# Keys made by features and turned back, edge features in two loads, borders for two steps at once

## The chip, the cores and the metric

The kernel runs on one core of a Trainium2 chip. The metric is the device time of one execution in microseconds (us); it is the time of that one core. TensorE (PE) multiplies and transposes, VectorE (DVE) and ScalarE (ACT) work elementwise, GpSimd (POOL) issues gathers, SyncE (SP) issues most of the other DMAs. An engine runs its instructions in program order and waits on semaphores for the others.

## What is computed

A graph of 12,500 nodes with 128 features and 212,500 edges that are sorted by their destination `dst`. Each edge has 128 features of its own. The layer, cut to what matters:

```python
h = relu(layernorm(x))                                   # nodes
q = h @ Wq.T + bq ;  v = h @ Wv.T + bv                   # nodes, 8 heads x 16
k = edge_attr @ Wk.T + bk                                # edges
in_m, out_m, diag_m = sum(q[src]*k), sum(q[dst]*k), sum(q[src]*q[dst])   # per edge and head
score = (segsoftmax(in_m/4) + segsoftmax(out_m/4) + segsoftmax(diag_m/4)) * edge_weight**lam
att = segment_sum(score * v[dst], dst)                   # score, for each node, times v
y = x + leaky_relu(att @ Wo.T + bo)
```

`segsoftmax` is a softmax over the edges of one destination node. Since `v[dst]` is the same for all edges of a node, the kernel sums only the scores.

## The kernel before, in words

All of it is in `ordered_path`. A prologue (to about 156 us of the profile) computes q of all nodes into a table in DRAM and starts the first gathers. Then comes one long loop, `for g in range(end)` at L1694, of 415 steps. The sorted edges are cut into S = 5 segments of G = 83 blocks of 512 edges; step g is segment s = g % 5 of block row t = g // 5. So five steps make one t, and some work is done once a t. The node work that can already be done is fitted in between, and a last part finishes the nodes.

Program order is fixed by hand: each `pin` ties an instruction behind the one pinned before it on its engine. One step g issues, in this order:

- `gather(g + LOOK)`, POOL, L712: four indirect DMAs of 128 rows of q each, 26 steps ahead. The first waits for the PE instruction noted as `behind[g, 0]`, the third for `behind[g, 2]`; both were noted a step earlier. This only keeps the gathers close behind the products.
- `fetch_edges(g + EDGES)`, SP, L692: the features `ea` of one step (128 x 512 float32, 256 KB), six buffers.
- `turn(g + 2)`: four PE transposes of `ea` into `eT_ps` (L1266, one PSUM buffer), ACT's copy to `eT` (L1268, three buffers).
- `one_hots(g + 3)`: two ACT instructions (L703, L704) that make the one-hot matrix `oh` of the edges' destinations.
- `project(g + 1)`: four float32 matmuls with a piece of `eT` as the stationary operand and `wk` moving (L1274) and a bfloat16 matmul of three rows by 512 columns that adds the bias (L1275), into `k_ps` (two PSUM buffers). The trace has two records for each of these float32 matmuls and one for each transpose, and a weight load (PEld) for each record.
- `spread_q(g + 1)`: four bfloat16 matmuls (L1282) that spread q of the destinations into `qd_ps` (two PSUM buffers), and ACT's copy `qd` (L1285).
- `logits(g)` on DVE: `qq*k_ps` (L1293), `qq*qd_ps` (L1294), `qd*k_ps` (L1295) into one buffer `prod`, and the sum over each head's 16 features (L1296) into `lT`.
- by s, work once a t for the steps of one or two t before: scans for the softmax (L1356, L1384), one-hots of segment ends, `to_rows` (L1452, L1457) and so on, and two further queues in SP's order, `fetch_rows` (`win`, L686) and `put_rows` (`sums`, L1473). `fetch(t + 2)` issues `relb` (L665, 630 KB) and the segments' borders `far` (L670, 135 KB, four buffers) once a t.

At the end of a step, `behind[g + 1, 2]` is set to the last PE instruction so far.

Of the kernel before, what the change touches and what calls it, by code (L numbers as in the profile page):

```python
# [472 lines left out]
def ordered_path(ctx: ExitStack, tc: tile.TileContext, flag, x, src, dst, edge_attr, edge_weight,  # L473
# [104 lines left out]
    bq_all = consts.tile([P, F], F32, name="bq_all")  # L578
    pin(nc.scalar.dma_start(bq_all, bq[None, :].to_broadcast([P, F])))
# [18 lines left out]
    bv3, bk3, bo3 = [b3[:, i, None, :].to_broadcast([3, JN, F]) for i in range(3)]  # L598
# [3 lines left out]
    K4 = 1 + S * JN  # L602
    show_end = consts.tile([K4, S * JN], F32, name="show_end")
# [47 lines left out]
    qqs, st, eas, behind, base_v = {}, {}, {}, {}, {}  # L651
# [5 lines left out]
    def fetch(t):  # L657
# [9 lines left out]
        far = load.tile([R, FB], BF, name="far", bufs=4)  # L667
        lo = t * FB + HEAD
        of = bass.AP(far_d.tensor, far_d.offset + lo, [[G * FB, S], [0, H3], [1, FB]])
        pin(nc.sync.dma_start(far, of))  # L670
# [18 lines left out]
    def fetch_edges(g):  # L689
        if g < end:  # L690
            ea = eas[g] = load.tile([P, JN * F], F32, name="ea", bufs=EDGES)
            pin(nc.sync.dma_start(  # L692
                ea, edge_attr[:end * BE, :].rearrange("(s b p j) f -> p s b (j f)", s=S, b=G, p=P)
                [:, g % S, g // S, :]))
# [101 lines left out]
    with tc.tile_pool(name="prep", bufs=1) as prep, \  # L796
# [249 lines left out]
        for g in range(EDGES):  # L1046
# [211 lines left out]
    with tc.tile_pool(name="work", bufs=2) as work, \  # L1258
            tc.tile_pool(name="scan", bufs=2) as scan, \
            tc.tile_pool(name="ps", bufs=1, space=PSUM) as ps:  # L1260
        ks, eTs, qds, q_ps, lTs = {}, {}, {}, {}, {}

        def turn(g):
# [3 lines left out]
            eT = work.tile([P, JN, P], F32, name="eT", bufs=3)  # L1267
# [3 lines left out]
        def project(g):  # L1271
            k_ps = ks[g] = ps.tile([P, JN, F], F32, name="k_ps", bufs=2)
            for j in range(JN):
                pin(nc.tensor.matmul(k_ps[:, j, :], eTs[g][:, j, :], wk, start=(j == 0), stop=False))  # L1274
            pin(nc.tensor.matmul(k_ps, ones3, bk3, start=False, stop=True))  # L1275
            del eTs[g]

        def spread_q(g):
            s, d = g % S, st[g // S]
            qd_ps = q_ps[g] = ps.tile([P, JN, F], F32, name="qd_ps", bufs=2)  # L1280
# [7 lines left out]
        def logits(g):  # L1288
# [3 lines left out]
            prod = work.tile([P, JN, 3, F], F32, name="prod", bufs=1)  # L1292
            pin(nc.vector.tensor_mul(prod[:, :, 0, :], qqs[g], ks[g]))  # L1293
            pin(nc.vector.tensor_mul(prod[:, :, 1, :], qqs[g], q_ps[g]))  # L1294
# [395 lines left out]
        project(0)  # L1690
        spread_q(0)
        turn(1)
        raw_rectify(SOON)
        for g in range(end):  # L1694
# [4 lines left out]
            fetch_edges(g + EDGES)  # L1699
            if s == 1:  # L1700
                load_sources(t + IDX)
            if g + 2 < end:
                turn(g + 2)
# [166 lines left out]
```

## Time and profile before

| | |
|---|---|
| median of 3 timed runs | 2671.06 us (2661.86 to 2672.03) |
| profiled execution | 2660.3 us, of it 2658.5 us span |
| mean granted TensorE clock | 0.756 |
| DMA | 357.03 MB, mean 134 GB/s |
| first and last sum over heads (L1296) start | 156.0 and 2596.9 us |
| last gather of the loop | about 2476 us |

The profiled execution is one run; its time is 10.8 us below the median of the timed runs. In the rows, `x415` is a number of instructions; after the bar stand busy time and the mean of one, after the second bar the time that the engine sat idle just before them, and what ended most of that. "remote" is a release that the trace can't put down to an instruction, "issue" is time in which the engine waited for nothing that the profile shows. PEclk is the granted clock, 1.00 or 0.50 in a short window and something between as a mean. A release put down to a PE instruction that had ended long before means that the signal, and not the instruction, came last.

### The profile page before, as it was taken

The numbers are of one execution on the slowest core, as the hardware profiler recorded it, in microseconds if no ns is written. First come the engines' busy times: TensorE is split into PE (matmuls) and PEld (weight loads), VectorE is DVE, ScalarE is ACT, GpSimd is POOL, SyncE is SP. The second block draws the span as 40 slices with busy tenths as digits, with TensorE's granted clock in tenths as the row PEclk, the third lists the DMA queues.
The fourth block names the chain that finished last, engine by engine and source line by source line (L and its number), as shares of the span: only waits on it lengthen the run. The fifth ranks groups of instructions, "written<-read, shape, count | busy, mean of one in ns | idle before, by whom it ended". The sixth has DMA issues, their size and how long they took to land.

```text
span 2658.5 us, 37037 instructions
## 1 busy us (share of the span) xinstructions
PE 1895.1 (71%) x10956; PEld 1466.7 (55%) x10956; DVE 2032.3 (76%) x2813; ACT 1406.8 (53%) x2743; POOL 1584.0 (60%) x1680
## 2 busy tenths in 40 slices
PE   4657866677677767777777767767767687777785
PEld 2446655555455555555555556545655565555564
DVE  4648878777777877777778777777877777777995
ACT  3647745554455555554555555545555555554672
POOL 6655666666666666666666666666666666666100
PEclk6777877776777777777777777777777777677886
DMA  7655445445545555455445444554455445454431
GB/s 197 191 163 150 127 133 143 129 135 139 146 131 144 134 147 135 136 141 141 119 130 139 128 129 130 135 137 122 123 140 135 127 127 135 134 131 122 126 88 53
DMA packets 379583, 357.03 MB, mean 134 GB/s; under 512 B 193216, under 2 KB 299371, under 8 KB 379167
## 3 DMA queue, kind: packets, MB, share of 16 engines
q1 hardware_dynamic: 310637, 239.38, 32.5%
q0 software_dynamic: 53152, 108.92, 16.4%
q10 hardware_dynamic: 15584, 6.27, 1.0%
q8 instruction: 90, 1.47, 0.2%
q14 instruction: 120, 0.98, 0.1%
HBM read 322.10 MB, written 32.22 MB: 133 GB/s over the span
## 4 chain that ended last, share of the span: by engine, by line
PE 48%; issue 14%; ACT 14%; DVE 12%; another core or an unknown queue 10%; DMA 1%; DVEq 1%; POOL 0%; SPq 0%; ACTq 0%
PE k_ps L1274 13%; PE eT_ps L1266 8%; PE w_ps L1452 6%; PE qd_ps L1282 4%; PE k_ps L1275 4%; ACT eT L1268 3%; ACT qd L1285 2%; PE m_ps L1396 2%; DVE lT L1296 2%; PE node_ps L1205 2%; ACT relb L703 2%; DVE prod L1294 2%; DVE prod L1293 1%; PE d_ps L1438 1%
## 5 line engine op out<-in xcount | busy, mean ns | idle before, releaser
L712 POOL DMA_INDIRECT qq<-q_table,sources x1564 | 1480.3, 946 | 852.7 <-issue 355.1
L1296 DVE TENSOR_REDUCE lT<-prod 128x96 f32<-128x1536 f32 x415 | 727.5, 1753 | 14.3
L1274 PE MATMUL k_ps<-wk,eT 128*128 128x128 f32 x3320 | 613.6, 343 | 70.5 <-issue 41.0
L1274 PEld LDWEIGHTS k_ps<-wk,eT 128*128 128x128 f32 x3320 | 562.0, 254 | 99.0 <-issue 54.2
L1266 PE MATMUL eT_ps<-ident,ea 128*128 128x128 f32 x1660 | 352.7, 347 | 349.7 <-issue 226.9
L1285 ACT COPY qd<-qd_ps 128x512 f32<-128x512 f32 x415 | 239.4, 577 | 533.7 <-remote 164.3
L1266 PEld LDWEIGHTS eT_ps<-ident,ea 128*128 128x128 f32 x1660 | 243.5, 177 | 441.1 <-issue 269.5
L1293 DVE TENSOR_TENSOR prod<-qq,k_ps 128x512 f32<-128x512 f32 x412 | 280.5, 681 | 186.6 <-remote 55.4
L1268 ACT COPY eT<-eT_ps 128x512 f32<-128x512 f32 x415 | 242.7, 585 | 252.9 <-remote 125.2
L1294 DVE TENSOR_TENSOR prod<-qq,qd_ps 128x512 f32<-128x512 f32 x412 | 281.4, 683 | 100.8 <-ACT qd L1285 55.0
L703 ACT ACTIVATE relb<-relb,before 126x512 bf16<-126x512 bf16 x415 | 302.6, 729 | 0.0
L1295 DVE TENSOR_TENSOR prod<-qd,k_ps 128x512 f32<-128x512 f32 x415 | 282.2, 680 | 0.0
L1452 PE MATMUL w_ps<-back,sel 128*126 128x144 f32 (+1 forms) x1296 | 209.5, 325 | 95.0 <-ACT sel L1442 59.2
L704 ACT ACTIVATE oh<-relb 126x512 bf16<-126x512 bf16 x415 | 261.4, 630 | 13.2
L1452 PEld LDWEIGHTS w_ps<-back,sel 128*126 128x126 f32 (+1 forms) x1296 | 190.7, 218 | 106.0 <-ACT sel L1442 66.2
L1282 PE MATMUL qd_ps<-win,oh 126*128 126x128 bf16 x1660 | 194.8, 248 | 12.6 <-issue 12.4
L1275 PE MATMUL k_ps<-b,ones 3*128 3x512 bf16 x415 | 192.6, 464 | 4.7 <-issue 4.7
L1282 PEld LDWEIGHTS <-oh 126*128 126x128 bf16 x1660 | 109.2, 107 | 141.7 <-issue 141.4
L1405 DVE TENSOR_TENSOR back<-lT,m_ps 128x480 f32<-128x480 f32 x83 | 54.1, 651 | 98.3 <-remote 37.7
L1356 DVE TENSOR_TENSOR_SCAN l_ps<-far,carry,l_ps 120x512 f32<-120x512 bf16 x80 | 102.5, 1282 | 20.1 <-PE h_ps L1324 10.2
L1396 PE MATMUL m_ps<-ident,m 120*128 120x120 f32 x332 | 72.4, 349 | 52.7 <-issue 38.1
L712 POOL DMA_INDIRECT qq<-in_x_dram,sources x84 | 81.7, 973 | 42.8 <-issue 22.2
(237 smaller groups left out, 1811.1 us busy)
## 6 DMA issues: line engine op xcount, KB each, us to landing
ea<-in_edge_attr_dram SPq DMA_DIRECT2D x415, 256.0 KB
relb<-rel_d SPq DMA_DIRECT2D x83, 630.0 KB
qq<-q_table,sources POOLq DMA_INDIRECT x1564
win<-q_table SPq DMA_DIRECT2D x415, 31.5 KB
far<-far_d SPq DMA_DIRECT2D x84, 135.0 KB
q_table<-q SPq DMA_DIRECT2D x24, 384.0 KB
sums<-rows SPq DMA_DIRECT2D x411, 7.9 KB
q_table<-xq SPq DMA_DIRECT2D x24, 256.0 KB
```

The source lines that it names most:

```text
L703: pin(nc.scalar.activation(d, d, AF.Abs, bias=before[:K3]))
L712: rows = pin(nc.gpsimd.indirect_dma_start(out=qq[:, j, :], out_offset=None, in_=x if g < RAW else q_table, in_offset=bass.IndirectOffsetOn ...
L1266: pin(nc.tensor.transpose(eT_ps[:, j, :], eas[g][:, j * F:(j + 1) * F], ident))
L1268: pin(nc.scalar.copy(eT, eT_ps))
L1274: pin(nc.tensor.matmul(k_ps[:, j, :], eTs[g][:, j, :], wk, start=(j == 0), stop=False))
L1275: pin(nc.tensor.matmul(k_ps, ones3, bk3, start=False, stop=True))
L1282: pin(nc.tensor.matmul(qd_ps[:, j, :], ohs[g][:, j * P:(j + 1) * P], d["win"][:, s, :], start=(j == 0), stop=(j == JN - 1)))
L1285: pin(nc.scalar.copy(qds[g], qd_ps))
L1293: pin(nc.vector.tensor_mul(prod[:, :, 0, :], qqs[g], ks[g]))
L1294: pin(nc.vector.tensor_mul(prod[:, :, 1, :], qqs[g], q_ps[g]))
L1296: pin(nc.vector.tensor_reduce(lTs[t][:, :, s, :], prod.rearrange("p j i (h d) -> p j (i h) d", d=DIM), AX.X, ALU.add))
L1452: pin(nc.tensor.matmul(w_ps[:(hi - lo) * W, lo:hi].rearrange("p s c -> p (s c)"), d["sel"][:n, j, lo:hi, :].rearrange("p s w -> p (s w)"), ...
```

## The change

- **k by features.** `project` becomes one float32 matmul of 128 x 512 with `wk` as the stationary operand and all four pieces of `eT` moving, into a new PSUM tile `kT_ps` (features by edges). ACT copies it to SBUF and adds the bias, which is now one number a partition (`bk_col`). A new step `turn_back` turns the four pieces back with PE transposes into `k_ps`. The bias matmul is gone.
- **Order and buffers.** One iteration now issues `turn_back(g + 1)`, `one_hots(g + 3)`, `spread_q(g + 1)`, `project(g + 2)`, `turn(g + 3)`, `fetch_edges(g + 6)`, `logits(g)`. `behind[g + 1, 0]` is noted behind `spread_q`. PSUM has eight banks, so `qd_ps` goes from two buffers to one to make room for `kT_ps`; `eT` goes from three to two. DVE now does `qq*qd_ps` ahead of `qq*k_ps`.
- **Edge features.** In place of five loads a t there are two: segments 0 to 2 (768 KB) and 3 to 4 (512 KB), each into one buffer of its own.
- **Borders.** `far` is loaded for two t at once, three buffers.

```diff
+    EA = {0: 3, 3: 2}
...
     def fetch(t):
...
-        far = load.tile([R, FB], BF, name="far", bufs=4)
-        lo = t * FB + HEAD
-        of = bass.AP(far_d.tensor, far_d.offset + lo, [[G * FB, S], [0, H3], [1, FB]])
-        pin(nc.sync.dma_start(far, of))
+        if t % 2 == 0:
+            n = min(2, T - t)
+            fars[t // 2] = load.tile([R, 2, FB], BF, name="far", bufs=3)
+            lo = t * FB + HEAD
+            of = bass.AP(far_d.tensor, far_d.offset + lo, [[G * FB, S], [0, H3], [1, n * FB]])
+            pin(nc.sync.dma_start(fars[t // 2][:, :n].rearrange("r b f -> r (b f)"), of))
+        far = fars[t // 2][:, t % 2]
...
     def fetch_edges(g):
-        if g < end:
-            ea = eas[g] = load.tile([P, JN * F], F32, name="ea", bufs=EDGES)
+        if g < end and g % S in EA:
+            n = EA[g % S]
+            ea = load.tile([P, n, JN * F], F32, name=f"ea_{n}", bufs=1)
+            for i in range(n):
+                eas[g + i] = ea[:, i]
...
-            eT = work.tile([P, JN, P], F32, name="eT", bufs=3)
+            eT = work.tile([P, JN, P], F32, name="eT")
...
         def project(g):
+            kT_ps = ps.tile([P, JN, P], F32, name="kT_ps", bufs=1)
+            pin(nc.tensor.matmul(kT_ps.rearrange("f j p -> f (j p)"), wk,
+                                 eTs.pop(g).rearrange("f j p -> f (j p)"), start=True, stop=True))
+            kTs[g] = work.tile([P, JN, P], F32, name="kT")
+            pin(nc.scalar.activation(kTs[g], kT_ps, AF.Identity, bias=bk_col))
+
+        def turn_back(g):
             k_ps = ks[g] = ps.tile([P, JN, F], F32, name="k_ps", bufs=2)
             for j in range(JN):
-                pin(nc.tensor.matmul(k_ps[:, j, :], eTs[g][:, j, :], wk, start=(j == 0), stop=False))
-            pin(nc.tensor.matmul(k_ps, ones3, bk3, start=False, stop=True))
-            del eTs[g]
+                pin(nc.tensor.transpose(k_ps[:, j, :], kTs[g][:, j, :], ident))
+            del kTs[g]
...
-            qd_ps = q_ps[g] = ps.tile([P, JN, F], F32, name="qd_ps", bufs=2)
+            qd_ps = q_ps[g] = ps.tile([P, JN, F], F32, name="qd_ps", bufs=1)
...
+            pin(nc.vector.tensor_mul(prod[:, :, 1, :], qqs[g], q_ps[g]))
             pin(nc.vector.tensor_mul(prod[:, :, 0, :], qqs[g], ks[g]))
-            pin(nc.vector.tensor_mul(prod[:, :, 1, :], qqs[g], q_ps[g]))
...
         for g in range(end):
...
-            fetch_edges(g + EDGES)
...
+            if g + 1 < end:
+                turn_back(g + 1)
+                one_hots(g + 3)
+                spread_q(g + 1)
+                behind[g + 1, 0] = pinned[products]
             if g + 2 < end:
-                turn(g + 2)
-            one_hots(g + 3)
-            if g + 1 < end:
-                project(g + 1)
-                behind[g + 1, 0] = pinned[products]
-                spread_q(g + 1)
+                project(g + 2)
+            if g + 3 < end:
+                turn(g + 3)
+            fetch_edges(g + EDGES)
             logits(g)
```

How the instructions stand in program order, first on PE, in the middle of the loop of the kernel before. One step is the transposes (L1266), the keys (L1274, L1275) and the spread q (L1282); behind it comes a row of the once-a-t work.

```order
2993 L1266 MATMUL eT_ps<-ident,ea 128x128 x4
2994 L1274 MATMUL k_ps<-wk,eT 128x128 x4
2995 L1275 LDWEIGHTS ones_90
2996 L1275 MATMUL k_ps<-b_96,ones_90 128x512
2997 L1282 LDWEIGHTS oh
2998 L1282 MATMUL qd_ps<-win,oh 128x128
2999 L1282 LDWEIGHTS oh
3000 L1282 MATMUL qd_ps<-win,oh 128x128
3001 L1282 LDWEIGHTS oh
3002 L1282 MATMUL qd_ps<-win,oh 128x128
3003 L1282 LDWEIGHTS oh
3004 L1282 MATMUL qd_ps<-win,oh 128x128
```

The same place on PE in the changed kernel (its lines are numbered anew: L1290 is `turn_back`, L1297 `spread_q`, L1282 `project`, L1275 `turn`).

```order
2766 L1290 MATMUL k_ps<-ident,kT 128x128 x4
2767 L1297 LDWEIGHTS oh
2768 L1297 MATMUL qd_ps<-win,oh 128x128
2769 L1297 LDWEIGHTS oh
2770 L1297 MATMUL qd_ps<-win,oh 128x128
2771 L1297 LDWEIGHTS oh
2772 L1297 MATMUL qd_ps<-win,oh 128x128
2773 L1297 LDWEIGHTS oh
2774 L1297 MATMUL qd_ps<-win,oh 128x128
2775 L1282 MATMUL kT_ps<-eT,wk 128x512
2776 L1275 MATMUL eT_ps<-ident,ea_12316 128x128 x4
```

What feeds DVE's next step (keys and spread q) now stands first in a step and the work for later steps behind it; the four key matmuls and the bias matmul with its weight load have become four transposes and one wide matmul.

SP's queue in the kernel before, from one fetch of borders to the next step but one (`ISA` and `TENSOR_LOAD` set up the DMA behind them):

```order
1331 L692 DMA ea<-in_edge_attr_dram 128x512
1332 L665 DMA relb<-rel_d 126x5x512
1333 L670 DMA far<-far_d 120x1x576
1334 L672 TENSOR_LOAD places
1335 L686 ISA
1336 L686 DMA win<-q_table 126x128
1337 L1473 ISA
1338 L1473 DMA sums_69<-rows 42x48
1339 L692 DMA ea<-in_edge_attr_dram 128x512
```

The same place in the changed kernel, in a t without a load of borders (L668 is `relb`, L692 `win`, L1488 `sums`, L701 the edge features):

```order
1134 L668 DMA relb<-rel_d 126x5x512
1135 L678 TENSOR_LOAD places
1136 L692 ISA
1137 L692 DMA win<-q_table 126x128
1138 L1488 ISA
1139 L1488 DMA sums_69<-rows 42x48
1140 L701 DMA ea_12041<-in_edge_attr_dram 128x3x512
1141 L692 ISA
```

The single loads of `ea` and every second `far` are gone from the queue, and one load of three segments stands behind `win` and `sums` of its step, where it waits for `turn` of that same step to free its buffer.

More of the change, by code (lines that the diff above doesn't have):

```diff
@@ L578, in ordered_path @@
     bq_all = consts.tile([P, F], F32, name="bq_all")
+    bk_col = consts.tile([P, 1], F32, name="bk_col")
+    pin(nc.scalar.dma_start(bk_col, bk[:, None]))
     pin(nc.scalar.dma_start(bq_all, bq[None, :].to_broadcast([P, F])))
@@ L597, in ordered_path @@
     b3 = consts.tile([3, 3, F], BF, name="b3")
-    bv3, bk3, bo3 = [b3[:, i, None, :].to_broadcast([3, JN, F]) for i in range(3)]
+    bv3, bo3 = [b3[:, i, None, :].to_broadcast([3, JN, F]) for i in (0, 2)]
     inv = consts.tile([P, NI], F32, name="inv")
@@ L649, in rows_in @@
         pin(q.dma_start(to[RW - 1:RW, :E - top], t[None, top:E]))
-    qqs, st, eas, behind, base_v = {}, {}, {}, {}, {}
+    qqs, st, eas, behind, base_v, fars = {}, {}, {}, {}, {}, {}
     def block_rows(t):
@@ L689, in fetch_edges @@
     def fetch_edges(g):
-        if g < end:
-            ea = eas[g] = load.tile([P, JN * F], F32, name="ea", bufs=EDGES)
+        if g < end and g % S in EA:
[3 more added lines that the diff above has]
+                eas[g + i] = ea[:, i]
             pin(nc.sync.dma_start(
                 ea, edge_attr[:end * BE, :].rearrange("(s b p j) f -> p s b (j f)", s=S, b=G, p=P)
-                [:, g % S, g // S, :]))
+                [:, g % S:g % S + n, g // S, :]))
     ohs = {}
@@ L1045, in ordered_path @@
             beside(2 * t - 4, load_sources, t)
-        for g in range(EDGES):
+        for g in range(S):
             beside(14 + g, fetch_edges, g)
@@ L1260, in ordered_path @@
             tc.tile_pool(name="ps", bufs=1, space=PSUM) as ps:
-        ks, eTs, qds, q_ps, lTs = {}, {}, {}, {}, {}
+        ks, kTs, eTs, qds, q_ps, lTs = {}, {}, {}, {}, {}, {}
         def turn(g):
@@ L1690, in ordered_path @@
         project(0)
+        turn(1)
+        turn_back(0)
         spread_q(0)
-        turn(1)
+        project(1)
+        turn(2)
+        fetch_edges(S)
         raw_rectify(SOON)
@@ L1810, in ordered_path @@
             halves_of(ab, engine)
-        places_o = [ps.tile([P, JN, F], F32, name="eT_ps", bufs=1)]
-        for r in range(2):
-            places_o += [ps.tile([P, JN, F], F32, name=name, bufs=2) for name in ("k_ps", "qd_ps")]
+        places_o = [ps.tile([P, JN, F], F32, name=name, bufs=n) for name, n in
+                    (("eT_ps", 1), ("kT_ps", 1), ("k_ps", 2), ("k_ps", 2), ("qd_ps", 1))]
         for r in range(len(rest) + 2):
```

## Prediction

> **What bounds the kernel now.** I read the page first, then the busy time by stretches, then the waits, then two short pieces of the timeline. No engine is full on the page:
>
> ```profile
> PE 1895.1 (71%) x10956; PEld 1466.7 (55%) x10956; DVE 2032.3 (76%) x2813; ACT 1406.8 (53%) x2743; POOL 1584.0 (60%) x1680
> PE 48%; issue 14%; ACT 14%; DVE 12%; another core or an unknown queue 10%; DMA 1%; DVEq 1%; POOL 0%; SPq 0%; ACTq 0%
> ```
>
> The busy time of two stretches, the loop proper and a piece behind the last gather (columns: PE, PEld, DVE, ACT, POOL with their instructions, clock, DMA):
>
> ```profile
> 300.00:2450.00 2150.00, 1550.69 (x8879) 1195.99 (x8877) 1671.38 (x2081) 1112.07 (x2118) 1375.18 (x1453) 0.75 0.51 134
> 2480.00:2590.00 110.00, 92.84 (x627) 73.52 (x627) 107.69 (x136) 80.55 (x163) 1.67 (x4) 0.86 0.36 101
> ```
>
> Without gathers DVE is busy 107.69 of 110 us: there the kernel runs as fast as DVE does its work. While gathers run DVE is busy only 78%, so something holds it that has to do with POOL. The groups of POOL and the waits of that stretch:
>
> ```profile
> L712 POOL DMA_INDIRECT qq<-q_table,sources x1453 | 1375.2, 946 | 772.8 <-issue 331.9 <-remote 136.7 <-PE qd_ps L1282 71.6
> POOL qq L712 <- issue: 331.9, 1082, 0.6
> ACT qd L1285 <- remote: 150.3, 52, 6.4
> ACT eT L1268 <- remote: 121.7, 60, 4.5
> DVE prod L1293 <- remote: 52.3, 30, 3.5
> PEld eT_ps L1266 <- ACT eT L1268: 136.7, 84, 6.7
> ```
>
> A gather takes 0.946 us and 0.31 of issue (331.9 / 1082) lie between two, so 1.25 us each; 1453 of them make 1820 us, and the other 330 of the 2150 us POOL waits. POOL in turn waits for PE, by `behind`. How, is seen at one place. POOL's rows in which it waited longer than the issue (the number in brackets is the idle time before), within one block row t:
>
> ```profile
> 564.59 0.94 POOL L712 DMA_INDIRECT qq<-q_table,sources  x1 [1.67 <-PE h_ps L1324]
> 573.41 0.94 POOL L712 DMA_INDIRECT qq<-q_table,sources  x1 [1.65 <-PE rest_ps L1572]
> 585.18 0.94 POOL L712 DMA_INDIRECT qq<-q_table,sources  x1 [2.07 <-PE eT_ps L1266]
> 593.99 0.94 POOL L712 DMA_INDIRECT qq<-q_table,sources  x1 [1.63 <-PE qd_ps L1282]
> ```
>
> From the first to the last are 29.40 us, the period of one t: 20 gathers of 1.25 us, 25.0, and three waits that are together 4.4 us longer than the issue. These are not waits for PE's work but for its signal. Another place in all engines:
>
> ```profile
> 1520.82 0.40 PE L1282 MATMUL qd_ps<-win,oh 126*128 126x128 bf16 x4
> 1521.05 0.69 PE L1396 MATMUL m_ps<-ident,m 120*128 120x120 f32 x4
> 1522.42 0.69 DVE L1293 TENSOR_TENSOR prod<-qq,k_ps 128x512 f32<-128x512 f32 x1 [1.92 <-PE m_ps L1396]
> 1522.48 0.59 ACT L1285 COPY qd<-qd_ps 128x512 f32<-128x512 f32 x1 [4.44 <-PE m_ps L1396]
> 1522.66 0.94 POOL L712 DMA_INDIRECT qq<-q_table,sources  x1 [1.63 <-PE m_ps L1396]
> 1523.61 1.12 PE L1266 MATMUL eT_ps<-ident,ea 128*128 128x128 f32 x4 [1.86 <-ACT eT L1268]
> 1530.03 0.59 ACT L1268 COPY eT<-eT_ps 128x512 f32<-128x512 f32 x1 [2.67 <-remote]
> ```
>
> ACT's copy of `qd_ps` begins at 1522.48, though its matmuls ended at 1521.22; DVE, ACT and POOL start within 0.24 us of each other, as if one signal had come for all. The transposes end by 1524.73, and ACT, idle, takes them at 1530.03. In the stretch without gathers the 2.3 us in which DVE is idle leave no room for such waits. My reading: while POOL works, PE's signals arrive late, and a pause of POOL lets them through. So the loop's length is POOL's 25.0 us a t plus about three such pauses, and the question is what the change does to the pauses.
>
> **The change, part by part.**
>
> ```profile
> L1274 PE MATMUL k_ps<-wk,eT 128*128 128x128 f32 x3320 | 613.6, 343 | 70.5 <-issue 41.0
> L1266 PE MATMUL eT_ps<-ident,ea 128*128 128x128 f32 x1660 | 352.7, 347 | 349.7 <-issue 226.9
> L1275 PE MATMUL k_ps<-b,ones 3*128 3x512 bf16 x415 | 192.6, 464 | 4.7 <-issue 4.7
> L1572 PE MATMUL rest_ps<-q_in,ident 128*128 128x512 f32 (+1 forms) x34 | 21.2, 712 | 2.9 <-issue 2.5 <-ACT hT L1200 0.4
> L987 PE MATMUL t_ps<-xq,ident 128*128 128x512 f32 x16 | 12.0, 842 | 0.0
> L1268 ACT COPY eT<-eT_ps 128x512 f32<-128x512 f32 x415 | 242.7, 585 | 252.9 <-remote 125.2
> L1285 ACT COPY qd<-qd_ps 128x512 f32<-128x512 f32 x415 | 239.4, 577 | 533.7 <-remote 164.3
> ```
>
> *PE's busy time.* A step loses the key matmuls, 613.6 / 415 = 1.48 us, and the bias, 0.46: 1.94. It gains one matmul of 128 x 512 (two records; 21.2 / 17 = 1.25 by L1572, 12.0 / 8 = 1.50 by L987) and four transposes, 352.7 / 415 = 0.85: 2.10 to 2.35. So +0.16 to +0.41 us a step, 66 to 170 us in all, beside PE's 28% of idle time in the loop: taken at 0. Without that cover it costs all of it, and at most that.
>
> *PE's instructions.* A step had 4 + 8 + 1 + 4 = 17 records and has 4 + 2 + 4 + 4 = 14, each with its weight load. The stretch shows 8879 records, 24.5 for each of 1453 / 4 = 363 steps; they become 21.5, 12% fewer. SP's DMAs fall as well: 415 loads of edge features become 166 and 84 of borders 42.
>
> *The late signals.* The pauses are 330 us in the stretch, so 356 over the loop from 156 to 2476. If their length goes with the instructions that are ahead of the signal, 12% is 43 us; if the loads count too, by the share of SP's issues, somewhat more. I take 14%, 50 us. The bounds: 0, if a pause belongs to the signals (as many in a step as before for the other work, one more for `kT`), and 123 us if three pauses a t become two (83 t of 4.4 / 3 us).
>
> *ACT.* One more copy a step with a bias, by the two rows of the same shape 0.58 us, 241 us in all; ACT goes from 53% to 62%. In order it sits between `qd` and `eT`, so when a late signal lets ACT go, PE gets `eT` 0.58 us later. PE waited for that copy 84 times in the stretch: 84 x 0.58 = 49 us, beside PE's idle time; taken at 0, with 49 as the bound.
>
> *One buffer of `qd_ps`.* `spread_q(g + 1)` now waits until DVE's `qq*qd_ps` and ACT's copy of step g have ended. Behind it in PE's queue are `project(g + 2)` and `turn(g + 3)`; DVE waits for it with the first product of the next step. By the rows below, from the end of that product DVE has 0.68 + 0.68 + 1.75 = 3.1 us of work left in the step, and four matmuls of 0.25 us and a signal have to fit in: 2.1 us spare when signals come at once. Taken at 0; it is the first rival.
>
> ```profile
> L1293 DVE TENSOR_TENSOR prod<-qq,k_ps 128x512 f32<-128x512 f32 x364 | 247.8, 681 | 182.1 <-remote 52.3 <-PE qd_ps L1282 31.2 <-PE m_ps L1396 28.7
> L1296 DVE TENSOR_REDUCE lT<-prod 128x96 f32<-128x1536 f32 x364 | 638.1, 1753 | 12.6
> L1282 PE MATMUL qd_ps<-win,oh 126*128 126x128 bf16 x1660 | 194.8, 248 | 12.6 <-issue 12.4
> ```
>
> *Loads.* SP itself, its longest waits and those of the edge loads:
>
> ```profile
> SPq L1473 <- ACT rows L1457: 387.5, 63, 11.2
> SPq L692 <- remote: 4.4, 11, 1.1
> ```
>
> Nobody waits for edge features now, and their loads wait 4.4 us in all: fewer loads save nothing by themselves. The load of three segments waits for `turn` of its own step and holds back the next step's `win` and `sums` behind it; the data is due three steps (18 us) later. SP already waits up to 11.2 us at `sums` without harm, so this is 0, and the same for `far`. The Trainium skill ("DMA: Bandwidth & Descriptors", its two cost components) gives each DMA a fixed cost of about 2 us; by it 291 fewer would be worth up to 582 us in a kernel that waits for them, an estimate from that page. The 4.4 us above say that this one does not.
>
> *The clock.* A quarter of a step's PE records are transposes now, and more than half after. Two short windows and the ones that follow them, and what PE did in the first and the third (L1316 and L1266 are transposes, L1452 is a float32 matmul):
>
> ```profile
> 472.10:475.51 3.41, 3.41 (x20) 3.41 (x19) 3.04 (x3) 0.00 (x0) 2.17 (x3) 0.50 0.15 40
> 475.51:478.93 3.42, 3.42 (x29) 2.66 (x28) 2.01 (x4) 2.62 (x8) 1.89 (x2) 1.00 0.34 105
> 1919.35:1922.76 3.41, 2.53 (x13) 2.27 (x12) 3.34 (x5) 3.35 (x7) 2.63 (x3) 0.50 0.53 146
> 1922.76:1926.17 3.41, 3.41 (x20) 3.41 (x19) 3.38 (x5) 0.41 (x1) 2.09 (x3) 0.50 0.15 38
> ```
> ```profile
> L1316 PE MATMUL l_ps<-ident,lT 128*120 128x128 f32 x4 | 1.1, 421 | 0.0
> L1266 PE MATMUL eT_ps<-ident,ea 128*128 128x128 f32 x4 | 1.1, 421 | 0.0
> L1452 PE MATMUL w_ps<-back,sel 128*126 128x144 f32 (+1 forms) x10 | 2.6, 444 | 0.9 <-ACT sel L1442 0.9
> ```
>
> A window that PE filled, 2.2 of 3.41 us of it with transposes, is followed by the full clock; one with 2.6 us of float32 matmuls and no transposes is followed by half. So transposes count here towards the clock, and the mix costs nothing: 0. The Trainium skill ("TensorE: Matmul & The Clock Gate", Part 4: PE-mode transpose) says that the full clock does not engage for transposes, which speaks against the change; these windows disagree with it.
>
> **The sum:** 2660.3 - 50 = 2610 us for an execution like the profiled one. The median of the timed runs is 10.8 us above it, so I forecast 2621 us. Its own range, from the bounds around the likely term (a gain of 15 to 85), is 2586 to 2656.
>
> **The rivals.**
>
> *The one-buffer `qd_ps` makes DVE wait (slower).* A late signal of 1.9 us as at 1522.42 already used up more than one step's lead. With 2.1 us spare, less the copy `qd` of 0.58 that the third product needs, what comes over 1.5 us late is DVE idle time. DVE has 1671.38 of 2150 us to do, 4.60 of 5.92 us a step, so it decides as soon as its waits are over 1.3 us a step on average; they are 1.3 now by definition, hidden in POOL's pace. Each of three late signals a t, 249 in all, that lets DVE lose 0.3 us more gives +75 us: 2746, and with 0.58 us each 2815. For it: the rows of L1285 and L1268 show how long signals stay away (up to 6.4 and 4.5 us). Against it: POOL's pace, not DVE's, is the longer one now.
>
> *No change.* The pauses are set by POOL's own gathers or by the number of signals, and POOL's 1.25 us and three pauses stay: 2671. For it: the waits come in the same rhythm whatever PE was doing (h_ps, rest_ps, eT_ps, qd_ps in the four rows). Against it: nothing direct.
>
> *A pause less.* With fewer instructions one of three pauses a t goes: -123 us, 2548. For it: DVE and ACT have room, as the stretch without gathers shows, where DVE alone sets the pace. Against it: 12% is less than a third.
>
> *The clock falls after all.* If transposes counted less than the windows show and the mean clock went from 0.756 to 0.70, PE's 1895 us would grow by 152, and by the 48% that PE has of the chain some 73 us would show: 2744. This is where the rule of the Trainium skill on the clock gate ("TensorE: Matmul & The Clock Gate", Part 4) would lead.
>
> *The loads are not early enough.* If the three-segment load lands late, `turn` waits once a t: 83 x 0.7 = 60 us, 2731. Against it: 18 us of lead.
>
> **How the numbers follow.** Forecast 0.40, one-buffer wait 0.22, no change 0.18, a pause less 0.13, clock 0.04, loads 0.03. Half a per cent, 13 us, is about what a measurement of this kernel can tell from no change. Faster by more than that: 0.40 + 0.13 = 0.53; within it 0.18; slower 0.22 + 0.04 + 0.03 = 0.29. The range leaves out the longer half of the first rival and the extreme of a pause less: 2530 to 2750.
>
> **What would show it.** Right: gathers still of 1.25 us, POOL's sum of waits in the loop at about 280 instead of 330 us in 2150, DVE over 79% busy there, PE's records at 28 a step with their weight loads, ACT at 62%. The clock stays at 0.75 or above, and `ea` is not waited for. Wrong: POOL's waits as before or longer, put down to `qd_ps`; DVE's wait ahead of its first product grown beyond 182 us; PE waiting for `kT`; a clock near 0.70. If POOL's share were the same and the time not, my account of what bounds the loop fails.

## The result and the profile after

The changed kernel takes 2676.1 us (median of 8 runs) against 2666.07 of the kernel before (8 runs): 1.0033 times as long, 95% interval 1.0022 to 1.0045. The forecast was 2621 us. So it is a third of a per cent slower, where the forecast had 1.9% faster (than the 2671.06 us known then).

The changed kernel's page, its busy times and the costliest groups that the change touches (L721 gathers, L1282 `project`, L1290 `turn_back`, L1275 `turn`, L1285 ACT's `kT`, L1308 and L1420 DVE's first product and `back`):

```profile
PE 1827.9 (68%) x9711; PEld 1267.7 (47%) x9711; DVE 2019.7 (76%) x2813; ACT 1657.1 (62%) x3158; POOL 1584.8 (59%) x1680
L721 POOL DMA_INDIRECT qq<-q_table,sources x1564 | 1480.7, 947 | 863.4 <-issue 363.5
L1282 PE MATMUL kT_ps<-eT,wk 128*128 128x512 f32 x830 | 609.0, 824 | 101.7 <-issue 60.9
L1290 PE MATMUL k_ps<-ident,kT 128*128 128x128 f32 x1660 | 329.7, 332 | 455.0 <-ACT kT L1285 307.0
L1285 ACT ACTIVATE kT<-kT_ps,bk_col 128x512 f32<-128x512 f32 x415 | 286.5, 690 | 141.4 <-issue 49.0
L1275 PE MATMUL eT_ps<-ident,ea 128*128 128x128 f32 x1660 | 320.5, 328 | 2.8 <-DVE att_t L877 2.8
L1308 DVE TENSOR_TENSOR prod<-qq,qd_ps 128x512 f32<-128x512 f32 x412 | 280.3, 680 | 175.2 <-ACT qd L1300 100.1
L1420 DVE TENSOR_TENSOR back<-lT,m_ps 128x480 f32<-128x480 f32 x83 | 54.2, 653 | 238.1 <-remote 99.5
```

On the page of before the last of these had waited 98.3 us:

```profile
L1405 DVE TENSOR_TENSOR back<-lT,m_ps 128x480 f32<-128x480 f32 x83 | 54.1, 651 | 98.3 <-remote 37.7
```

The two stretches of the changed kernel (PE, PEld, DVE, ACT, POOL, clock, DMA), and its POOL in the first of them:

```profile
300.00:2450.00 2150.00, 1477.52 (x7786) 1012.90 (x7784) 1655.77 (x2077) 1329.07 (x2478) 1372.87 (x1451) 0.80 0.50 133
2480.00:2590.00 110.00, 87.48 (x535) 63.06 (x533) 104.21 (x132) 89.81 (x173) 6.37 (x9) 0.89 0.39 109
```
```profile
L721 POOL DMA_INDIRECT qq<-q_table,sources x1451 | 1373.6, 947 | 780.4 <-issue 338.8 <-remote 129.6 <-PE qd_ps L1297 60.6
```

PE has the 12% fewer records that were forecast (7786 in place of 8879) and a higher clock (0.80 in place of 0.75). ACT has its 62%. And the loop is as long as before: 1451 gathers in 2150 us in place of 1453, and the pauses, worked out as in the prediction (2150 less 1451 x (0.947 + 0.311)), are 325 us in place of 330. PE's idle time did not go but changed its place, and grew by 73 us in the stretch (1550.69 us busy before, 1477.52 now). Before it stood ahead of `turn`, 349.7 us in the whole run, where now 2.8 us are left; now it stands ahead of `turn_back`, 455.0 us. The waits of the stretch, of POOL, of PE, and of ACT ahead of its copies:

```profile
POOL qq L721 <- issue: 338.8, 1090, 1.2
PEld k_ps L1290 <- ACT kT L1285: 322.8, 128, 7.0
PE k_ps L1290 <- ACT kT L1285: 288.2, 121, 6.8
ACT qd L1300 <- remote: 141.5, 39, 6.0
ACT eT L1277 <- remote: 94.3, 34, 5.7
```

A single signal of PE is as late as before: ACT's longest waits are 6.0 and 5.7 us, where they were 6.4 and 4.5. They are fewer (39 and 34, where they were 52 and 60) and somewhat shorter in sum (141.5 and 94.3 us, where they were 150.3 and 121.7), but ACT also has 217 us more of work to fill them with, and neither POOL's pauses nor the loop became shorter. From the timeline of the changed kernel:

```profile
1503.03 0.59 ACT L1277 COPY eT<-eT_ps 128x512 f32<-128x512 f32 x1 [4.94 <-remote]
1503.27 0.94 POOL L721 DMA_INDIRECT qq<-q_table,sources  x1 [2.14 <-remote]
...
1503.67 2.07 PE L1282 MATMUL kT_ps<-eT,wk 128*128 128x512 f32 x2 [4.43 <-ACT eT L1277]
...
1506.39 1.01 PE L1411 MATMUL m_ps<-ident,m 120*128 120x120 f32 x4
1507.43 0.65 DVE L1420 TENSOR_TENSOR back<-lT,m_ps 128x480 f32<-128x480 f32 x1 [5.66 <-issue]
...
1508.74 0.40 PE L1297 MATMUL qd_ps<-win,oh 126*128 126x128 bf16 x4 [0.84 <-DVE back L1420]
...
1511.88 0.59 ACT L1300 COPY qd<-qd_ps 128x512 f32<-128x512 f32 x1 [1.88 <-PE d_ps L1453]
1512.12 0.94 POOL L721 DMA_INDIRECT qq<-q_table,sources  x1 [1.66 <-PE d_ps L1453]
1512.37 0.69 ACT L1285 ACTIVATE kT<-kT_ps,bk_col 128x512 f32<-128x512 f32 x1
1512.95 0.59 ACT L1277 COPY eT<-eT_ps 128x512 f32<-128x512 f32 x1
```

Twice POOL and ACT start together after a wait; the second time the matmuls of `qd_ps` had ended at 1509.14, 2.7 us earlier, and ACT has three copies to do in a row where it had two. DVE's wait of 5.66 us at `back` is not a late signal: the matmuls of `m_ps` themselves end only at 1507.40, since ahead of them PE had waited 4.43 us for ACT's `eT`.

### The profile page after: what moved, and what is told of

It is laid out like the page before. It is cut to its first block, busy times and chain, and to the rows that moved or that the text cites. A ratio compares the mean times of both kernels' runs of the same rounds, so it can differ in the third digit from the quotient of the medians.

```text
span 2673.1 us, 34936 instructions
## 1 busy us (share of the span) xinstructions
PE 1827.9 (68%) x9711; PEld 1267.7 (47%) x9711; DVE 2019.7 (76%) x2813; ACT 1657.1 (62%) x3158; POOL 1584.8 (59%) x1680
## 4 chain that ended last, share of the span: by engine, by line
PE 40%; ACT 19%; DVE 15%; issue 11%; another core or an unknown queue 11%; DMA 2%; DVEq 1%; POOL 1%; ACTq 0%; SPq 0%; POOLq 0%
PE kT_ps L1282 13%; PE k_ps L1290 6%; PE eT_ps L1275 5%; PE qd_ps L1297 4%; ACT kT L1285 4%; ACT qd L1300 3%; DVE lT L1311 3%; PE w_ps L1467 3%; ACT relb L712 3%; DVE prod L1308 3%; PE node_ps L1214 2%; ACT eT L1277 2%; DVE prod L1310 2%; DVE prod L1309 2%
## 5 line engine op out<-in xcount | busy, mean ns | idle before, releaser
L721 POOL DMA_INDIRECT qq<-q_table,sources x1564 | 1480.7, 947 | 863.4 <-issue 363.5
L1282 PE MATMUL kT_ps<-eT,wk 128*128 128x512 f32 x830 | 609.0, 824 | 101.7 <-issue 60.9
L1290 PE MATMUL k_ps<-ident,kT 128*128 128x128 f32 x1660 | 329.7, 332 | 455.0 <-ACT kT L1285 307.0
L1290 PEld LDWEIGHTS k_ps<-ident,kT 128*128 128x128 f32 x1660 | 226.8, 168 | 532.3 <-ACT kT L1285 347.0
L1275 PEld LDWEIGHTS eT_ps<-ident,ea 128*128 128x128 f32 x1660 | 269.6, 175 | 324.7 <-issue 312.8
L1308 DVE TENSOR_TENSOR prod<-qq,qd_ps 128x512 f32<-128x512 f32 x412 | 280.3, 680 | 175.2 <-ACT qd L1300 100.1
L1285 ACT ACTIVATE kT<-kT_ps,bk_col 128x512 f32<-128x512 f32 x415 | 286.5, 690 | 141.4 <-issue 49.0
L1275 PE MATMUL eT_ps<-ident,ea 128*128 128x128 f32 x1660 | 320.5, 328 | 2.8 <-DVE att_t L877 2.8
L1297 PE MATMUL qd_ps<-win,oh 126*128 126x128 bf16 x1660 | 198.2, 254 | 136.2 <-DVE prod L1308 86.2
L1420 DVE TENSOR_TENSOR back<-lT,m_ps 128x480 f32<-128x480 f32 x83 | 54.2, 653 | 238.1 <-remote 99.5
L1297 PEld LDWEIGHTS <-oh 126*128 126x128 bf16 x1660 | 149.3, 115 | 178.8 <-DVE prod L1308 83.7
L1282 PEld LDWEIGHTS kT_ps<-eT,wk 128*128 128x128 f32 x830 | 165.7, 248 | 112.9 <-issue 67.0
L1467 PE MATMUL w_ps<-back,sel 128*126 128x144 f32 (+1 forms) x1296 | 162.8, 281 | 8.9 <-ACT sel L1457 4.3
L1467 PEld LDWEIGHTS w_ps<-back,sel 128*126 128x126 f32 (+1 forms) x1296 | 156.9, 186 | 12.6 <-ACT sel L1457 6.6
L721 POOL DMA_INDIRECT qq<-in_x_dram,sources x84 | 82.1, 978 | 41.8 <-issue 22.5
```

Source lines behind the costliest of these rows:

```text
L721: rows = pin(nc.gpsimd.indirect_dma_start(out=qq[:, j, :], out_offset=None, in_=x if g < RAW else q_table, in_offset=bass.IndirectOffsetOn ...
L1275: pin(nc.tensor.transpose(eT_ps[:, j, :], eas[g][:, j * F:(j + 1) * F], ident))
L1282: pin(nc.tensor.matmul(kT_ps.rearrange("f j p -> f (j p)"), wk, eTs.pop(g).rearrange("f j p -> f (j p)"), start=True, stop=True))
L1285: pin(nc.scalar.activation(kTs[g], kT_ps, AF.Identity, bias=bk_col))
L1290: pin(nc.tensor.transpose(k_ps[:, j, :], kTs[g][:, j, :], ident))
L1297: pin(nc.tensor.matmul(qd_ps[:, j, :], ohs[g][:, j * P:(j + 1) * P], d["win"][:, s, :], start=(j == 0), stop=(j == JN - 1)))
```

## The experiments

Each run stands beside the kernel before on the same chip, and the chips differ: in the experiments the kernel before took 2664 to 2696 us on four chips and 2186 us on a fifth. Ratios are to the kernel before on the same chip. "Late" and "prompt" below are these two kinds of chip.

**On the chip with prompt signals (before: 2186.42 us): loads alone, keys alone, half of the gathers.** The first run has only the new loads (the edge loads behind `turn(g + 2)` with `fetch_edges(g + 5)`), the second only the rest of the change. In the other two a step in two gathers nothing and uses the rows of the step before, so part of the result is not computed:

```diff
+            if g > 60 and g % 2:
+                qqs[g] = qqs[g - 1]
+                return
             qq = qqs[g] = firsts[g] if g < FIRST else gath.tile([P, JN, F], F32, name="qq")
```

> The kernel before with only the loads changed: edge features in two loads a block row, borders for two block rows at once; the keys are made as before. First theory (a part of the change gains and another part takes it back, and the loads are what takes): 30 to 60 us slower than before. Second theory (the loop's length is POOL's gathers plus pauses that neither the loads nor PE's instructions set): within 10 us of before. Third theory (the forecast's, late signals go with the number of PE's and SP's instructions): 5 to 15 us faster.

Measured: 2185.66 us, 0.9995 (0.9985 to 1.0004).

> The changed kernel with the old loads (five loads of edge features a block row, borders for each block row): only the keys by features, the new order and the one buffer of qd_ps are left of the change. First theory (the loads take back what the keys gain): 30 to 50 us faster than before. Second theory (gathers plus pauses that PE's instructions do not set): within 15 us of before. Third theory (late signals go with PE's instructions): 43 us faster.

Measured: 2194.44 us, 1.0039 (1.0025 to 1.0053).

> The kernel before, in which from step 61 on every second step gathers nothing and uses the rows of the step before it; half of the gathers are left out, so part of the result is not computed. Second theory (POOL's gathers and what they do to PE's signals set the pace): a step falls from 5.9 us to near DVE's 4.6 us, some 1.2 us x 350 = 420 us faster, near 2250. First theory with hand-offs between PE, ACT and DVE as the bound: no change or under 100 us faster.

Measured: 2131.31 us, 0.9748 (0.9729 to 0.9768).

> The changed kernel with the same half of the gathers left out. Second theory: near the run of the kernel before with half the gathers, within 20 us, since DVE sets the pace of both. First theory (one buffer of qd_ps or ACT's extra copy costs time that the gathers hide): over 40 us slower than that run.

Measured: 2171.27 us, 0.9931 (0.9911 to 0.9951).

The expectations had been written for a kernel of 2666 us. Here POOL issues gather on gather: in the loads run its gathers and the gaps of 0.30 us between them fill the stretch (1212.5 + 388.4 us of 1600). DVE is nearly full too, in the loads run 96% and in the keys run 97% of the stretch:

```profile
L719 POOL DMA_INDIRECT qq<-q_table,sources x1274 | 1212.5, 952 | 388.4 <-issue 258.8 <-DMA qq<-q_table,sources 26.2 <-PE qd_ps L1289 18.3
```
```profile
300.00:1900.00 1600.00, 1290.54 (x8346) 999.74 (x8347) 1541.45 (x1957) 1024.81 (x1992) 1211.93 (x1274) 0.83 0.60 164
```
```profile
300.00:1900.00 1600.00, 1211.92 (x7314) 843.74 (x7314) 1546.71 (x1958) 1248.46 (x2336) 1210.53 (x1276) 0.90 0.64 165
```

So the pace is that of POOL's own gathers with DVE close behind it, and PE's fewer records (7314 in place of 8346 for as many gathers) have nothing to give. Nor is a signal late: of the 342 copies of `qd_ps` that start in that stretch of the loads run, none starts over 0.6 us after its four matmuls and ACT's instruction before it had ended; in the kernel before on the chip of the prediction 121 of 271 start over 1 us after that, up to 6.1. What DVE waits for, in the loads run and in the keys run, and in the keys run PE:

```profile
DVE prod L1300 <- DMA qq<-q_table,sources: 25.9, 13, 3.8
```
```profile
DVE back L1414 <- PE m_ps L1405: 21.5, 28, 1.2
DVE prod L1302 <- ACT qd L1294: 9.3, 11, 1.1
PE qd_ps L1291 <- DVE prod L1302: 319.3, 248, 5.2
```

In the old order of PE the once-a-t transposes `m_ps` are done in time; in the new one DVE waits for them, since ahead of them PE waits at `spread_q` for DVE's product. These are waits of the kind that the first rival names. Whether the one buffer or the new order makes them was not separated on this chip. The keys run is 8 us longer, but DVE does not idle more in this stretch than in the loads run, where it waits for gathered rows instead. With half of the gathers, where DVE no longer waits for gathered rows, the same waits show: before and after are 40 us apart (2171 against 2131), at the edge of what the first theory had said.

**The change again, and two tries at its new waits (before: 2666.4 us, late).** The unaltered change, the change with DVE's first two products in the old order, and the change with two buffers of `qd_ps` that `kT_ps` pays for:

```diff
-            kT_ps = ps.tile([P, JN, P], F32, name="kT_ps", bufs=1)
+            kT_ps = ps.tile([P, JN, P], F32, name="kT_ps", tag="eT_ps", bufs=1)
...
-            qd_ps = q_ps[g] = ps.tile([P, JN, F], F32, name="qd_ps", bufs=1)
+            qd_ps = q_ps[g] = ps.tile([P, JN, F], F32, name="qd_ps", bufs=2)
```

> The changed kernel unaltered, on the chip of this call. The kernel before took 2666 us where the change was timed and 2186 us on the chip of the last call, so this shows which of the two levels this call has. Theory of the one buffer (the new wait of spread_q for DVE's product, and what stands behind it on PE, costs DVE 8 to 10 us a run): 0.3 to 0.5% slower than before on either level. Theory of pauses set by PE's instructions: slower only where signals are not late, and 1 to 2% faster where they are.

Measured: 2676.46 us, 1.0035 (1.0019 to 1.0051).

> The changed kernel with DVE's first two products in the old order, qq*k_ps first. Theory of the one buffer: qd_ps is freed 0.68 us later in a step, so PE's spread_q and all behind it start 0.68 us later; PE waits more for DVE, and DVE's wait at back for m_ps grows: 10 to 40 us slower than the changed kernel. Rival (what costs is that DVE's first product now waits for ACT's copy of qd): 5 to 10 us faster than the changed kernel, as fast as before.

Measured: 2675.45 us, 1.0039 (1.0028 to 1.0051). Neither theory: the order of the products does nothing.

> The changed kernel with two buffers of qd_ps again, paid for by letting kT_ps share the one buffer of eT_ps, so that turn of a step waits until ACT has copied the kT before it. Theory of the one buffer: PE no longer waits for DVE at spread_q, DVE's waits at back and at the first product go, and the time is 10 to 40 us below the changed kernel where signals are prompt. Rival (ACT's extra copy and the longer chain turn, copy, project, copy, turn back cost it): the same as the changed kernel or slower, since the shared buffer makes that chain longer still.

Measured: 2906.39 us, 1.0926 (1.0884 to 1.0967). The rival: the hand-offs turn, copy, project, copy follow one another without lead now, and late signals stand between them. PE's wait for it in the loop:

```profile
PE eT_ps L1275 <- ACT kT L1285: 538.0, 233, 6.2
```

**More and fewer PE records (late).** Six more small matmuls a step, and, on another late chip (before: 2663.66 us), the old keys with bfloat16 operands (`eT` copied to bfloat16, a bfloat16 copy of `wk`), one record a matmul in place of two.

```diff
             qd_ps = q_ps[g] = ps.tile([P, JN, F], F32, name="qd_ps", bufs=2)
+            for j in range(6):
+                pin(nc.tensor.matmul(qd_ps[:, 0, :8], ohs[g][:, j % JN * P:(j % JN + 1) * P],
+                                     d["win"][:, s, :8], start=True, stop=True))
```

> The kernel before with six more small matmuls a step (126 x 128 stationary, 8 columns) with their weight loads ahead of spread_q, into a place that spread_q overwrites: 12 more records a step, 25% more, and some 0.7 us of PE. Theory that late signals go with the number of PE's instructions: where signals are late (before at about 2666 us) 80 to 90 us slower. Theory that PE's instructions set nothing there: within 15 us. Where signals are prompt (before at about 2186 us) PE has 17% idle and DVE sets the pace: within 15 us by either, or up to 100 us slower if PE comes to bound it.

Measured: 2702.48 us, 1.0142 (1.0119 to 1.0165).

> The kernel before with eT and Wk in bfloat16 for the keys: one record in place of two for each of the four matmuls, so 8 of 49 records fewer a step with their weight loads, less PE time, and no added hand-off. Theory that lateness goes with PE's records: where signals are late 24 us (by the 3 us a record of the run with twelve more) to 57 us (by proportion) faster than before. Theory that only hand-offs count: within 10 us. Where signals are prompt DVE sets the pace: within 10 us.

Measured: 2649.56 us against 2663.66, 0.9947 (0.9929 to 0.9965).

Both lie between their two theories. 36 us for twelve records and 14 for eight are 3.0 and 1.8 us for each record a step, PE's time for them included. By that the change's six fewer (three matmuls and three weight loads) are worth 11 to 18 us, an estimate from these two runs, not 50.

**Half of the gathers where signals are late, the keys alone, the keys a step earlier (before: 2663.66 us).** The third run is the change with `project(g + 3)` and `turn(g + 4)`, three buffers of `kT`.

> The kernel before with every second step's gathers left out (part of the result is not computed), as in the run on the chip where signals were prompt (2131 us there). On a chip where the kernel before takes about 2666 us: if POOL's gathers are what makes PE's signals late, near 2131 to 2250 us; if signals are late on that chip whatever POOL does, over 2500 us. On a chip where it takes about 2186 us: 2131 us again.

Measured: 2184.11 us, 0.8201 (0.8183 to 0.8219), 480 us less. In its stretch DVE is busy 97%:

```profile
300.00:2150.00 1850.00, 1523.94 (x9853) 1180.12 (x9852) 1789.69 (x2285) 1207.46 (x2344) 731.23 (x770) 0.83 0.52 140
```

So it is the gathers that hold the loop on these chips, through something other than their own time: half of the gathers leave 1.25 x 10 = 12.5 us a block row on POOL, and little is left of the lateness. From 560 to 1900 us 29 of 293 copies of `qd_ps` start over 1 us late, by 2.2 us at most. The pace is that of the prompt chip: from the sum over heads of step 100 to that of step 380 it takes 1283.6 us (677.60 to 1961.21), with half of the gathers on the prompt chip 1281.1 (626.62 to 1907.75). The 53 us between the two runs lie ahead of step 61, where all gathers are still issued.

> The changed kernel with the old loads, as in the run where signals were prompt (0.4% slower there). Where signals are late: theory that the fewer PE records and the added hand-off over ACT (kT) cancel: within 10 us of the changed kernel, 0.3 to 0.5% slower than before, so the loads do nothing. Rival (the loads' wait for PE on SP costs there): 10 us or more faster than the changed kernel.

Measured: 2683.26 us, 1.0085 (1.0063 to 1.0107): slower than the whole change on the chip before (1.0035, up to 1.0051). So where signals are late the loads seem to do something: by the two ratios, of two chips, about half a per cent. The loads alone were not run on a late chip.

> The changed kernel with project and turn one step earlier (project(g + 3), turn(g + 4), three buffers of kT), so that ACT's copy kT has one more step before PE turns it back. Theory that the added hand-off took back what fewer PE records gained: where signals are late PE's wait for kT (325 us in the loop of the changed kernel) falls to under 150 us and the time to 18 to 60 us below the changed kernel, faster than before. Rival (the gathers' pace with pauses is the bound whatever PE does): no change from the changed kernel within 10 us. Where signals are prompt: within 10 us of the changed kernel.

Measured: 2682.99 us, 1.0072 (1.0055 to 1.0088). The wait for `kT` is gone from the list of PE's waits, and another stands there:

```profile
PE qd_ps L1297 <- DVE prod L1308: 268.9, 119, 7.8
```

In the changed kernel that row had 69.0 us. PE waits elsewhere, and the time does not fall: the rival, though by the ratios of two chips it is even some 0.4% longer than the change.

**What a pause of POOL is (before: 2664.29 us, late).** In one run a memset of 128 x 64 on POOL follows every gather, in the other the gathers do not wait for `behind`:

```diff
                 held = None
+                if g >= 60:
+                    pin(nc.gpsimd.memset(spacer, 0.0))
```
```diff
-                if held is not None:
+                if False:
                     tc.add_manual_dep(rows.ins, held, mybir.DependencyInfo(
```

> The kernel before with a small memset of 128 x 64 on POOL behind every gather from step 60 on, so that gathers start further apart and POOL issues no DMA for a moment after each. Where signals are late: theory that PE's signals get through when POOL issues no gather, 1.25 us a gather become some 1.45 but the three pauses a block row (4.4 us) shrink, 20 x 0.2 = 4.0 against 4.4: within 30 us of before, with POOL's long waits for PE (over 1.3 us) fewer by half or more. Theory that pauses belong to PE's own work, not to POOL's issue: they stay, and the time grows by 83 x 4.0 = 330 us. Where signals are prompt: POOL's 29 us a block row come above DVE's 24, so up to 350 us slower.

Measured: 2669.37 us, 1.0020 (1.0008 to 1.0032). POOL in the loop, and ACT's waits there:

```profile
L713 POOL DMA_INDIRECT qq<-q_table,sources x1451 | 1391.1, 959 | 529.7 <-issue 207.2 <-remote 124.9 <-PE qd_ps L1285 55.0
L724 POOL MEMSET spacer<- 128x64 f32 x1394 | 234.7, 168 | 1.0
ACT qd L1288 <- remote: 185.2, 61, 9.5
ACT eT L1271 <- remote: 146.4, 60, 7.5
```

The memset takes the place of half the issue gap, so a gather with all around it takes 0.959 + 0.168 + 207.2 / 1188 = 1.30 us, only 0.05 more than before. Over 1451 gathers that is about 70 us; the pauses fall from 330 to 262, and the time stays. So a pause is what others leave over of the period. The memsets do not let signals through: ACT waits for them no less than before, where the two rows had 150.3 us in 52 waits and 121.7 in 60, and POOL's waits of over 1.3 us fall only from 174 to 135, not to the half that was expected.

> The kernel before in which the gathers no longer wait for PE's products (behind); they wait only until the buffer that they write has been read, as they do anyway. Where signals are late: theory that POOL's pauses are what lets signals through: POOL then runs without pauses to the end of its buffers, signals stay away for longer, and the time is over 50 us longer, with longer single waits at ACT and DVE. Rival (the pauses themselves are the cost, 25.0 us a block row are POOL's floor): up to 300 us faster. Where signals are prompt: within 20 us.

Measured: 2957.42 us, 1.1116 (1.1088 to 1.1145). Who waits now, in the loop:

```profile
POOL qq L712 <- DVE prod L1294: 458.7, 120, 6.0
ACT qd L1285 <- remote: 340.7, 65, 9.5
```

Before, ACT waited there 150.3 us in 52 times, 6.4 at the longest. POOL runs on until its buffers are full, and PE's signals stay away for longer. The short waits of POOL are not the cost; without them it is 293 us more, 57 of them ahead of the first sum over heads, which starts at 212.7 us in place of 156.0.

**Pieces of the key part, one by one (late).** One buffer of `qd_ps` in the kernel before; one more ACT instruction of 128 x 512 behind the copy `eT`; one tiny ACT copy out of `k_ps` (before: 2695.88 us for this last one):

```diff
             pin(nc.scalar.copy(eT, eT_ps))
             eTs[g] = eT
+            spare = work.tile([P, JN, P], F32, name="spare")
+            pin(nc.scalar.activation(spare, eT, AF.Identity, bias=eps))
```
```diff
             pin(nc.tensor.matmul(k_ps, ones3, bk3, start=False, stop=True))
+            spare = work.tile([P, 8], F32, name="spare")
+            pin(nc.scalar.copy(spare, k_ps[:, 0, :8]))
```

> The kernel before with one buffer of qd_ps in place of two and nothing else. Theory that the one buffer is what takes back the gain of the keys: where signals are late 20 to 40 us slower than before; where they are prompt 8 to 40 us slower. Rival (the added PE, ACT, PE hand-off or ACT's extra copy): within 10 us of before.

Measured: 2665.49 us, 1.0006 (0.9995 to 1.0018).

> The kernel before with one more ACT instruction of 128 x 512 a step behind the copy eT (it writes a tile that nobody reads): ACT's extra work of the change, 0.6 to 0.7 us a step, without its hand-off to PE. Theory that ACT's work takes back the gain: where signals are late 20 to 40 us slower. Rival (one buffer, or the hand-off): within 10 us. Where signals are prompt: within 10 us.

Measured: 2678.28 us, 1.0054 (1.0037 to 1.0071).

> The kernel before with a tiny ACT copy (128 x 8) out of k_ps behind the bias matmul of each step: one more signal from PE to ACT a step for which ACT waits in order, and k_ps is free only after it, without the 0.6 us of work. Where signals are late: theory that the added hand-off takes back what ACT's extra work (14 us) does not explain: 10 to 30 us slower than before. Rival (the hand-off costs nothing, PE's half clock or its order does): within 8 us. Where signals are prompt: within 8 us.

Measured: 2703.61 us, 1.0025 (1.0011 to 1.0039).

One buffer costs nothing here, in the old order. ACT's extra instruction costs 14 us (10 to 19 by the interval), between its theory and its rival. A further signal for ACT to wait for, with the 0.155 us of the small copy, costs 7 us: the rival's range. It is not ACT alone that waits there; the trace puts waits of DVE's first product down to the small copy:

```profile
DVE prod L1295 <- ACT spare L1277: 205.3, 114, 4.2
```

**A version from the pieces that did not cost time (before: 2695.88 us, late).** The kernel before with the change's loads and bfloat16 keys.

> The kernel before with the two pieces that gained or cost nothing: the loads of the change (two of edge features a block row, borders for two block rows) and bfloat16 keys by edges with eight PE records fewer a step. Where signals are late: if the two add up, 14 us for the keys and some 7 for the loads, 15 to 25 us faster than before, so 25 to 35 us faster than the changed kernel. Rival (the loads' gain needs the new order): 14 us faster. Where signals are prompt: within 10 us of before.

Measured: 2664.61 us, 0.9877 (0.9857 to 0.9898), 31 us below the kernel before, more than the 15 to 25 that were expected: better than either kernel, since the change is 0.35% above it. Its keys are less exact than float32 ones.

## Why the prediction was wrong

The step that failed is the one on **the late signals**: "If their length goes with the instructions that are ahead of the signal, 12% is 43 us", taken as 50. The instructions went down by the 12%, the pauses from 330 to 325 us. Two things in that step did not hold. A record a step is worth 1.8 to 3.0 us, so by estimate six are 11 to 18 us. And the sum itself, 25.0 us of POOL's work and pauses that come on top, was no sum: with spaced gathers the work grew and the pauses shrank by as much (262 us), and without holding the gathers the time grew by 293 us. What I had read rightly is that the gathers hold PE's signals back (480 us less with half of them), and that DVE, ACT and POOL wait for signals and not for work. What I made of it, that a pause is a cost in proportion to PE's records, was a reading of rows in which POOL's wait and its reason stand side by side. The signs agree: DVE is busy 77% of the stretch and not over 79%, the pauses are as before, and PE waits for `kT` (288.2 us), which had been named as a sign of being wrong.

Of the rivals *no change*, with a chance of 0.18, came nearest: 2671 us, with POOL's 1.25 us and the three pauses as they were. They stayed in this change. But they are not fixed, as the spaced gathers show, and the result is clear of no change, if only by a third of a per cent.

*PE's busy time.* The exchange was sized rightly: 609.0 + 329.7 us in place of 613.6 + 192.6, 132 us more, within the 66 to 170. It does not show in the sum, which is 67 us less (1827.9 in place of 1895.1), as other instructions became shorter at the higher clock (`turn` 320.5 in place of 352.7 us). It lay beside idle time, as forecast.

*ACT.* The 62% came, though the instruction with the bias took 0.69 us and not 0.58 (286.5 us in all, not 241). The cost was not 0: three copies stand in a row after a late signal, and 14 us (1.0037 to 1.0071) is what one more instruction costs by itself, within the bound of 49. The added hand-off cost 7 us in a run of its own.

*One buffer of `qd_ps`*, the rival with the largest chance, does nothing alone on a late chip (1.0006). On the prompt chip, where DVE is nearly full, the new order with it costs DVE its waits at `back`; the keys as a whole cost 8 us there, and the whole change 40 without the gathers' own limit, not 75 or more.

*The loads.* `ea` was not waited for, as forecast, though SP now waits for `turn` ahead of the edge loads, as its queue in the changed kernel shows:

```profile
SPq L701 <- PE eT_ps L1275: 205.1, 39, 9.9
```

That they save nothing held on the prompt chip (0.9995). Where signals are late the change without them is half a per cent slower than with them, by ratios of two chips, so there the new loads seem to be a gain, and I had put it inside the wrong term. The 2 us that the prediction quotes from the Trainium skill ("DMA: Bandwidth & Descriptors", the two cost components) stand there under the path of DMAs that GpSimd issues, while these are SP's; no term of the sum rests on them.

*The clock* rose from 0.756 to 0.80 with twice the transposes, and fell to 0.63 (0.61 in the stretch) with bfloat16 keys and the same transposes as before:

```profile
300.00:2450.00 2150.00, 1391.90 (x7491) 971.97 (x7488) 1667.07 (x2092) 1114.48 (x2138) 1382.38 (x1463) 0.61 0.51 134
```

The rule of the Trainium skill ("TensorE: Matmul & The Clock Gate", Part 4: PE-mode transpose), by which transposes do not engage the full clock, does not hold for these float32 transposes. The two means alone would not show it, since the change also widened the key matmuls. But the two windows of the prediction are not alone: in the trace of the kernel before, the clock keeps one value over stretches of 3.41 us or multiples of them. Of the stretches with 0.8 to 1.5 us of other float32 matmuls and under 0.3 us of transposes 4 of 56 are followed by the full clock, of those with over 0.9 us of transposes 66 of 90. And the clock did not set the time here: the kernel with 0.63 is the shorter one.

*What is left open.* Added up for the late chips, the pieces of the key part are 14 + 7 + 0 - (11 to 18), 3 to 10 us; measured alone it is 17 to 28 us slower (1.0063 to 1.0107). The rest is not settled. The way back, PE waiting for ACT's `kT`, is not it by itself, since giving it a step more of lead took that wait away and saved nothing. Nor is it shown that such pieces add.

## What to carry to other kernels

When engines wait for a signal long after the work is done, find out first what holds the signal, by taking half of the suspect away; the waits themselves, and the engine that pauses last, are not a budget from which a change can be paid. A change that trades instructions on an engine with idle time for one more hand-off gained nothing here, where hand-offs are what is late, and hand-offs without lead cost 9%. Run the kernel before beside every experiment: what was bound by late signals on four chips ran at the pace of its gathers, with DVE nearly full, on the fifth.

## What the runs showed of the hardware

- The same kernel took 2664 to 2696 us on some chips and 2186 on another, with gathers of the same length (0.946 us, and 0.952 in the loads run) and a clock of 0.76 against 0.82. On the latter PE's signals come at once though the gathers run: none of 342 copies of `qd_ps` starts over 0.6 us late, where 121 of 271 start over 1 us late on one of the former. What differs between the chips is open.
- On the former chips gathers on POOL hold back PE's signals, by what way is open: half of them left out take 480 us away, and ACT's copy of `qd_ps` waited 150 us in 52 waits with the gathers held behind PE, and 341 us in 65 without.
- Float32 transposes count towards the granted clock (66 of 90 stretches with them are followed by the full clock, 4 of 56 without), and bfloat16 matmuls in place of float32 ones brought the mean down to 0.63.
